# A gated cross-attention and mixture-of-experts layer: shorter gate logarithm, other places for state update and router products, idle products in the first tiles

## The chip, the core and the metric

The kernel runs on one core of a Trainium2 chip. The metric is the device time of one execution in microseconds (us); lower is better. The core has five engines with a queue each: PE (TensorE, matmuls and transposes), DVE (VectorE), ACT (ScalarE), POOL (GpSimd) and SP (SyncE, here only an issuer of DMAs). Each queue runs in order, so an instruction that waits holds up everything behind it on its engine.

## The reference, cut to what matters

Two residual layers over 8 x 512 tokens of 1024 float32 numbers. The first is an mLSTM with 16 heads of 64; q is the normalised x, k and v are the context:

```python
ig, fg = cat(q, k, v) @ Wi + bi, cat(q, k, v) @ Wf + bf      # one number a head and token
log_D = tril(cumsum(log_sigmoid(fg)) differences) + ig
D = exp(log_D - max_log_D)
C = (q k^T / 8) * D;  h = C / max(|sum C|, exp(-max_log_D)) @ v   # then a norm over each head
x = x + tanh(g_xattn) * hn
logits = layernorm(x) @ router_w.T                            # 16 experts, the best 2 of them
x = x + tanh(g_ffn) * (shared(layernorm(x)) + sum of the 2 experts)
```

`shared` and every expert are `silu(y @ gate) * (y @ up) @ down`, 1024 wide inside for the shared one and 512 for an expert.

## The kernel before, in words

Tokens go in 32 tiles of 128 (`NT = 32`), four tiles to a sequence (`NS = 4`). The work has two stages. The **loop over tiles** (the body of `flamingo_layer` from L848 on, the steps `for i in range(1, NT)`) does the mLSTM of tile i, the norm of tile i-1 and its router, and the preparation of tiles i+1 and i+2; into the gaps of PE it puts `Unit`s of the shared expert for finished tiles (`fill`, L253 gate and up products, L275 down products). The **expert stage** after it (from about 1460 us on) gathers rows by expert and multiplies (L1346). The change lies in the loop only.

A step i consists of these pieces:

- `prep_queries`, `prep_keys` (L446/L447) transpose the normalised row and the context of tile i+1; `gate_products` (L454) multiplies both by the gate weights.
- `prep_gates(i+1)`: one product `pg` (L502), then a chain on 16 x 128 numbers that goes to and fro between DVE and ACT: bias, `exp(-|f|)`, `u = 1 + z`, `ln u`, a correction by division (L519 to L527, with a RECIPROCAL at L522), two scans (`cum` L531, `m` L535) and `nm` (L539). It then writes `nm` and `e = exp(..)` to DRAM and reads them back spread over partitions: `d` (L543, L544, 128 x 2048) and, for tiles that are not the first of their sequence, `eb` (L551, L554).
- `prep_columns(i+1)` transposes the gate rows (L568, evacuated by DVE at L570), masks `d` on POOL (L573), takes `decay` out of `eb` and scales `eb` by the queries on DVE (L579, L580), and makes `wv` on POOL (L588).
- `scores`, `prep_weights` and `values` make the attention of tile i (L624, L631, L615, L652, and L646 for the state of earlier tiles). `scores`, `values` and `grow` share the two buffers of PSUM tag "a".
- `grow(i)` brings the state up to date: POOL scales it by `decay` (L667), PE makes `pst` (L675), DVE adds it (L684; L682 for a first tile). Only when DVE has read `pst` is its PSUM buffer free for the next `scores`.
- `head_scale(i)` (L692 to L700), `head_norm`, `finish_rows` end a tile; `turn_rows(i-1)` transposes the finished row into `yT` (two copies at L447, one on ACT, one on DVE); `route_products(i-1)` multiplies `yT` by the router (L454, `pp<-yT,rwT`), `finish_route` adds its parts (L745).
- Once in four tiles `place_group` computes slots and POOL issues eight indirect DMAs into `table_d` (L825).

The text order sets priorities. A scheduler fixes the order of each engine's queue at build time; `tc.issue_after(ins)` forces an instruction behind another on its engine. Before, the order on PE around the change is in most steps: `yT` transposes, one unit, router products, `values` 2 and 3, `grow` with a little of a unit between its halves, `pl`, `pc`, a unit, transposes of the next queries, `scores`.

In the first 60 us tile 0 goes through all of this with no shared expert to fill waits. Its loads are issued by SP and by ACT (L351 to L355, L395, L417, L434).

Of the kernel before, what the change touches and what calls it, by code (L numbers as in the profile page):

```python
# [9 lines left out]
F32 = mybir.dt.float32  # L10
# [36 lines left out]
def flamingo_layer(  # L47
# [274 lines left out]
    with ExitStack() as actx:  # L322
# [16 lines left out]
        def load_kv(i: int):  # L339
            q, b, c = toks[i], i // NS, i % NS  # L340
            q.kv = wk.tile([P, D], F32, tag="kv", name="kv")
            nc.sync.dma_start(q.kv, ctx_in[b, c * P : (c + 1) * P, :])
# [10 lines left out]
        bias_f = ac.tile([NH, 1], F32, name="bias_f")  # L353
        nc.scalar.dma_start(bias_i, bi.unsqueeze(1))
        nc.scalar.dma_start(bias_f, bf.unsqueeze(1))  # L355
        ones_p = ac.tile([P, P], F32, name="ones_p")
# [37 lines left out]
        lnsc = ac.tile([P, D], F32, name="lnsc")  # L394
        nc.scalar.dma_start(lnsc, ln_scale.unsqueeze(0).to_broadcast([P, D]))  # L395

# [19 lines left out]
        zeros = state.rearrange("p c e -> p (c e)")  # L416
        nc.scalar.dma_start(acc_d[T : T + P, :], zeros[:, :D])  # L417
        zero80 = ac.tile([P, NT_], F32, name="zero80")
# [12 lines left out]
        def prep_router():  # L431
            nc.vector.tensor_scalar(lnsc, lnsc, tgx, None, ALU.mult)
            rw = wk.tile([NE, D], F32, tag="u", name="rw", bufs=1)
            nc.scalar.dma_start(rw, router_w)  # L434
            nc.vector.memset(rwT, 0.0)
            prw = ps.tile([P, NC, NE], F32, tag="tr", name="prw")
            for c in range(NC):
                nc.tensor.transpose(prw[:, c, :], rw[:, c * P : (c + 1) * P], ident[:NE, :NE])
            nc.scalar.copy(rwT[:, :, 0:NE], prw)

        def transposed(dst, src_of, copies):
# [55 lines left out]
        def prep_gates(i: int, after=()):  # L497
            q, last, first = toks[i], i % NS == NS - 1, i % NS == 0
            pg = ps.tile([48, P], F32, tag="tr", name="pg")
            with ExitStack() as order:  # L500
                pinned(order, after)
                nc.tensor.matmul(pg, lhsT=sums, rhs=q.parts, start=True, stop=True)  # L502

            def row(name, bufs=2):
                return gt.tile([NH, P], F32, tag=name, name=name, bufs=bufs)

            f = row("f", 1)
            a, en, w = (rows3[i % 2][32 * k : 32 * k + NH, :] for k in range(3))
            nc.scalar.copy(f, pg[32:48, :])
            nc.vector.tensor_scalar(a, pg[0:NH, :], bias_i, None, ALU.add)  # L510
            nc.vector.tensor_scalar(f, f, bias_f, None, ALU.add)


            z, u, lnu, eq = (row(n, 1) for n in ("z", "u", "lnu", "eq"))
            nc.vector.scalar_tensor_tensor(z, f, -1.0, f, ALU.mult, ALU.min)
            nc.scalar.activation(z, z, AF.Exp)
            nc.vector.tensor_scalar(u, z, 1.0, None, ALU.add)
            nc.scalar.activation(lnu, u, AF.Ln)
            nc.vector.tensor_scalar(u, u, -1.0, None, ALU.add)  # L519
            nc.vector.tensor_scalar(eq, u, 0.0, None, ALU.is_equal)  # L520
            nc.vector.tensor_add(u, u, eq)
            nc.vector.reciprocal(u, u)  # L522
            nc.vector.tensor_mul(u, u, z)
            nc.vector.tensor_mul(lnu, lnu, u)
            nc.vector.tensor_mul(eq, eq, z)
            nc.vector.tensor_add(lnu, lnu, eq)
            nc.vector.scalar_tensor_tensor(f, f, 0.0, lnu, ALU.min, ALU.subtract)  # L527

# [33 lines left out]
            if not last:  # L562
                nc.scalar.activation(w, a, AF.Exp, bias=nm[:, P - 1 : P])

        def prep_columns(i: int):
            q, last, first = toks[i], i % NS == NS - 1, i % NS == 0
            pc = ps.tile([P, 5, NH], F32, tag="tr", name="pc")
# [3 lines left out]
            if i > 0:  # L571
# [4 lines left out]
                ).ins  # L576
            if not first:
                q.decay = sm.tile([P, NC], F32, tag="decay", name="decay", bufs=2)
                nc.vector.tensor_copy(q.decay, q.eb[:, :, P - 1])  # L579
                nc.vector.scalar_tensor_tensor(  # L580
                    q.eb, q.eb, DH**-0.5, q.qT, ALU.mult, ALU.mult
                )
            if not last:
# [152 lines left out]
        def route_products(i: int):  # L736
            q = toks[i]
            q.parts = in_groups(rwT, lambda c: q.yT[:, c, :], NC)
# [110 lines left out]
        load_kv(1)  # L849
        prep_norm(0)  # L850
        prep_queries(0)
        prep_keys(0)
# [3 lines left out]
        gate_products(0)  # L856
        prep_gates(0)
        prep_columns(0)
        with tc.issue_after(normed.last):
# [16 lines left out]
        prep_gates(1)  # L876
        grow(0)
        turn_rows(0)
        for k in range(8):
# [14 lines left out]
        for i in range(1, NT):  # L894
# [20 lines left out]
            if nxt:  # L915
                gate_products(i + 1)
            scored = scores(i, 1)
            if nxt:
                prep_gates(i + 1, scored)
# [17 lines left out]
            fill(share)  # L937
            if back:
                route_products(i - 1)
            values(i, 2)  # L940
            valued = values(i, 3)
            head_scale(i)
            if not last:
                grow(i)
            if i + 2 < NT:
                load_kv(i + 2)
            fill(share)
            if back:
                whole = finish_route(i - 1, valued)
            if nxt:  # L950
# [599 lines left out]
```

## Time and profile before

| what | us |
|---|---|
| median of 3 runs (lowest to highest) | 3169.66 (3166.38 to 3173.43) |
| the profiled execution | 3181.43 |
| its span, first to last instruction | 3179.4 |
| PE busy in the span | 3056.6 |
| DVE, ACT, POOL busy | 1793.8, 864.4, 1296.7 |
| mean granted TensorE clock | 0.978 |

The span by stage, from the busy time in stretches:

| stretch, us | length | PE busy | granted clock | DVE busy |
|---|---|---|---|---|
| 0 to 100 | 100 | 66.58 | 0.80 | 52.61 |
| 100 to 260 | 160 | 141.75 | 0.93 | 101.23 |
| 260 to 1420 | 1160 | 1114.96 | 0.97 | 777.88 |
| 1420 to 1480 | 60 | 50.17 | 0.91 | 17.69 |
| 1480 to 3179 | 1699 | 1683.16 | 1.00 | 844.42 |

Length less PE busy is time in which PE had nothing to do. Where the granted clock is under 1, PE was busy but slower: at 0.5 a matmul takes about twice as long. An "idle before, releaser" entry in a row names what ended the wait.

### The profile page before, as it was taken

The page shows a single profiled execution, that of the slowest core. Times are in us where ns is not written, and L with a number is a line of the kernel's source. Part 1 is how long each engine was busy: PE and PEld are TensorE (multiplying, and loading weights), DVE is VectorE, ACT ScalarE, POOL GpSimd, SP SyncE. Part 2 cuts the span into 40 slices and gives each one's busy share as a digit, 9 for nine tenths or more (in the row PEclk, how much of TensorE's full clock was granted, in tenths as well). Part 3 has the DMA queues.
Part 4 walks back from the last instruction along what each step waited for, and adds up shares of the span by engine and source line. Part 5 has one row for each costly group of instructions (what it writes and reads, how often), then busy time and mean ns, then how long its engine had stood idle before and what let it go on. Part 6 is the DMA issues. An engine that isn't in the chain of part 4 may idle for free.

```text
span 3179.4 us, 42509 instructions
## 1 busy us (share of the span) xinstructions
PE 3056.6 (96%) x16193; PEld 2289.5 (72%) x16193; DVE 1793.8 (56%) x3597; ACT 864.4 (27%) x1824; POOL 1296.7 (41%) x1019
## 2 busy tenths in 40 slices
PE   6889999899999999998999999999999999999999
PEld 5778677686877768676666677777777777767776
DVE  5656676676766766653444444444554554555554
ACT  3544444453545445411111111111111111100000
POOL 2212232322232222316555555565665545444442
PEclk7999999998999999999999999999999999999999
DMA  6776565565656565545544444454545544644330
GB/s 190 211 223 182 179 189 178 172 187 159 189 176 206 169 184 179 172 142 202 136 131 115 136 132 135 134 141 134 141 139 138 148 118 133 211 159 159 113 126 27
DMA packets 371103, 500.59 MB, mean 157 GB/s; under 512 B 24304, under 2 KB 263072, under 8 KB 366768
## 3 DMA queue, kind: packets, MB, share of 16 engines
q1 hardware_dynamic: 342560, 425.00, 42.2%
q0 software_dynamic: 24576, 71.52, 10.7%
q8 instruction: 130, 2.13, 0.3%
q10 hardware_dynamic: 3760, 1.31, 0.2%
q14 instruction: 77, 0.63, 0.1%
HBM read 394.57 MB, written 113.69 MB: 160 GB/s over the span
## 4 chain that ended last, share of the span: by engine, by line
PE 50%; DVE 4%; issue 0%; DVEq 0%
PE pq L1346 47%; PE ptx L1264 2%; DVE hsum L1414 1%; PE pq L1453 1%; DVE hT L1368 1%; DVE hsum L1415 1%; DVE up L1367 0%; DVE tsum L1295 0%; DVE tsum L1292 0%; DVE tsum L1293 0%; DVE yo L1425 0%; DVE xT L1267 0%; DVE u L1432 0%; DVE hT L1416 0%; DVE u L1431 0%
## 5 line engine op out<-in xcount | busy, mean ns | idle before, releaser
L1346 PE MATMUL pq<-xT,w 128*128 128x256 f32 (+12 forms) x2112 | 498.3, 386 | 9.0 <-DVEq L1327 9.0
L1346 PEld LDWEIGHTS pq<-xT,w 128*128 128x128 f32 x2112 | 402.5, 191 | 84.1 <-issue 20.2
L1346 PE MATMUL pq<-tsum,wsum 128*128 128x256 f32 (+12 forms) x1408 | 339.4, 384 | 0.0
L275 PE MATMUL pso<-sh_down,sh_hT 128*128 128x512 f32 x640 | 294.9, 605 | 2.5 <-DVE sh_base L281 2.5
L1346 PEld LDWEIGHTS pq<-tsum,wsum 128*128 128x128 f32 x1408 | 264.2, 190 | 39.7
L253 PE MATMUL pgu<-sh_yT,swg 128*128 128x256 f32 (+1 forms) x1280 | 287.5, 377 | 5.3 <-issue 4.2
L253 PE MATMUL pgu<-sh_yT,swu 128*128 128x256 f32 (+1 forms) x1280 | 285.3, 375 | 0.5 <-DMA swu<-n_L_ffn_shared_up_w_dram 0.5
L118 POOL TENSOR_SCALAR ve<-bmv 128x1 f32<-128x1 f32 x64 | 17.3, 270 | 590.8 <-DVE bmv L130 584.8
L253 PEld LDWEIGHTS pgu<-sh_yT,swg 128*128 128x128 f32 x1280 | 231.5, 193 | 36.4 <-issue 6.4
L253 PEld LDWEIGHTS pgu<-sh_yT,swu 128*128 128x128 f32 x1280 | 230.9, 192 | 31.8 <-issue 2.7
L1370 DVE TENSOR_TENSOR hT<-pq,u 128x256 f32<-128x256 f32 (+12 forms) x176 | 75.7, 430 | 300.5 <-PE pq L1346 280.7
L1311 POOL TENSOR_TENSOR wsum<-w 128x512 f32<-128x512 f32 x88 | 113.6, 1290 | 278.9 <-PE pq L1346 277.6
L275 PEld LDWEIGHTS pso<-sh_down,sh_hT 128*128 128x128 f32 x640 | 117.1, 192 | 124.7 <-issue 118.8
L1367 DVE TENSOR_TENSOR up<-pq,u 128x256 f32<-128x256 f32 (+12 forms) x176 | 75.6, 430 | 211.7 <-PE pq L1346 210.4
L1069 POOL DMA_INDIRECT acc_d<-yo,row_i x64 | 102.1, 1595 | 189.8 <-ACT yo L1443 81.5
L1346 PE MATMUL pq<-wd,hT 128*128 128x512 f32 x352 | 170.0, 598 | 7.1 <-DVE hT L1368 5.4
L1346 PE MATMUL pq<-xT,wsum 128*128 128x256 f32 (+12 forms) x704 | 169.6, 384 | 0.0
L1346 PE MATMUL pq<-tsum,w 128*128 128x256 f32 (+12 forms) x704 | 169.6, 384 | 0.0
L1346 PE MATMUL pq<-dsum,hT 128*128 128x512 f32 x352 | 165.4, 592 | 0.0
L1346 PE MATMUL pq<-dsum,hsum 128*128 128x512 f32 x352 | 165.4, 592 | 0.0
L1425 DVE TENSOR_TENSOR yo<-pq,u 128x512 f32<-128x512 f32 x176 | 119.3, 688 | 81.6 <-PE pq L1346 69.0
L1371 ACT ACTIVATE hT<-hT 128x256 f32<-128x256 f32 (+12 forms) x176 | 74.1, 421 | 327.9 <-DVE hT L1370 327.9
(274 smaller groups left out, 5462.3 us busy)
## 6 DMA issues: line engine op xcount, KB each, us to landing
swg<-L_ffn_shared_gate_w_dram SPq DMA_DIRECT2D x88, 512.0 KB, 5.2
swu<-n_L_ffn_shared_up_w_dram SPq DMA_DIRECT2D x88, 512.0 KB, 5.8
w<-in_L_ffn_gate_w_dram SPq DMA_DIRECT2D x16, 2048.0 KB, 10.8
w<-in_L_ffn_up_w_dram SPq DMA_DIRECT2D x16, 2048.0 KB, 10.6
wd<-in_L_ffn_down_w_dram SPq DMA_DIRECT2D x16, 2048.0 KB, 7.9
d<-nm_d SPq DMA_DIRECT2D x31, 1024.0 KB, 6.2
x_sb<-in_x_dram SPq DMA_DIRECT2D x32, 512.0 KB, 4.8
kv<-in_ctx_dram SPq DMA_DIRECT2D x32, 512.0 KB, 6.3
```

Source lines behind the costliest of these rows:

```text
L253: last = nc.tensor.matmul(pg[:, half, :n], lhsT=st[k][half][:, c, :], rhs=st["yT"][:, c, :n], start=(c == 0), stop=(c == NC - 1),)
L275: last = nc.tensor.matmul(po, lhsT=st["hT"][:, k, t * P : (t + 1) * P], rhs=sh_down[:, k, cols], start=(k == 0), stop=(k == 2 * NFC - 1),)
L1069: nc.gpsimd.indirect_dma_start(out=rows, out_offset=bass.IndirectOffsetOnAxis(ap=index, axis=0), in_=row, in_offset=None, compute_op=ALU.add,)
L1264: nc.tensor.transpose(pt[:, c, :], row[:, (half * 4 + c) * P : (half * 4 + c + 1) * P], ident)
L1311: nc.gpsimd.tensor_tensor(s1, a21, a22, ALU.add)
L1346: nc.tensor.matmul(out, lhsT=left[:, c, :], rhs=right[:, c, :], start=(c == 0), stop=(c == chunks - 1))
L1367: nc.vector.tensor_tensor(up, part, other, ALU.add)
L1368: nc.vector.tensor_tensor(out, out, up, ALU.mult)
L1370: nc.vector.tensor_tensor(out, part, other, ALU.add)
L1371: nc.scalar.activation(out, out, AF.Silu)
L1414: nc.vector.tensor_tensor(s1, a21, a22, ALU.add)
L1425: nc.vector.tensor_tensor(rows[t][:, halves[half]], part, other, ALU.add)
```

## The change

- **Gates.** The correction of the logarithm becomes `((u - 1) - z)`, added, with no division: three DVE instructions (new L528 to L530) in place of nine (L519 to L527); ACT adds the bias of `f` while it copies it (L518), so that one more DVE instruction goes, and the tile `eq`.
- **State inputs.** `decay` and the scaling of `eb` move from `prep_columns(i+1)`, at the end of step i, to a new `prep_state(i)` after the second half of `scores(i)`.
- **Order in a step.** `grow(i)` stands ahead of `head_scale(i)`. `route_products(i-1)` stands behind both and is forced behind the last product of `values(i, 3)`; `finish_route(i-1)` is forced behind the last unit put in (`behind`) in place of the last product of `values`.
- **Idle products.** `keep_awake(n)` issues n products of two constants, whose result nothing reads: 24 after the norm of tile 0, 26 behind `pg` of tile 0, 30 behind `pg` of tile 1.
- **Loads.** Five small loads and stores at the start go from ACT's queue to POOL's; `kv` has three buffers instead of two.

```diff
-            q.kv = wk.tile([P, D], F32, tag="kv", name="kv")
+            q.kv = wk.tile([P, D], F32, tag="kv", name="kv", bufs=3)
...
-        nc.scalar.dma_start(bias_i, bi.unsqueeze(1))
-        nc.scalar.dma_start(bias_f, bf.unsqueeze(1))
+        nc.gpsimd.dma_start(bias_i, bi.unsqueeze(1))
+        nc.gpsimd.dma_start(bias_f, bf.unsqueeze(1))
...
-        nc.scalar.dma_start(lnsc, ln_scale.unsqueeze(0).to_broadcast([P, D]))
+        nc.gpsimd.dma_start(lnsc, ln_scale.unsqueeze(0).to_broadcast([P, D]))
...
-        nc.scalar.dma_start(acc_d[T : T + P, :], zeros[:, :D])
+        nc.gpsimd.dma_start(acc_d[T : T + P, :], zeros[:, :D])
...
-            nc.scalar.dma_start(rw, router_w)
+            nc.gpsimd.dma_start(rw, router_w)
...
+        def keep_awake(n: int, after=None):
+            idle = ps.tile([P, P], F32, tag="o", name="idle")
+            with ExitStack() as order:
+                if after is not None:
+                    order.enter_context(tc.issue_after(after))
+                for _ in range(n):
+                    nc.tensor.matmul(idle, lhsT=ident, rhs=ones_p, start=True, stop=True)
...
-            nc.scalar.copy(f, pg[32:48, :])
+            nc.scalar.activation(f, pg[32:48, :], AF.Identity, bias=bias_f)
             nc.vector.tensor_scalar(a, pg[0:NH, :], bias_i, None, ALU.add)
-            nc.vector.tensor_scalar(f, f, bias_f, None, ALU.add)
...
             nc.scalar.activation(lnu, u, AF.Ln)
-            nc.vector.tensor_scalar(u, u, -1.0, None, ALU.add)
-            nc.vector.tensor_scalar(eq, u, 0.0, None, ALU.is_equal)
-            nc.vector.tensor_add(u, u, eq)
-            nc.vector.reciprocal(u, u)
-            nc.vector.tensor_mul(u, u, z)
-            nc.vector.tensor_mul(lnu, lnu, u)
-            nc.vector.tensor_mul(eq, eq, z)
-            nc.vector.tensor_add(lnu, lnu, eq)
-            nc.vector.scalar_tensor_tensor(f, f, 0.0, lnu, ALU.min, ALU.subtract)
+            nc.vector.scalar_tensor_tensor(u, u, -1.0, z, ALU.add, ALU.subtract)
+            nc.vector.scalar_tensor_tensor(f, f, 0.0, u, ALU.min, ALU.add)
+            nc.vector.tensor_sub(f, f, lnu)
...
+        def prep_state(i: int):
+            q = toks[i]
+            if i % NS == 0:
+                return
+            q.decay = sm.tile([P, NC], F32, tag="decay", name="decay", bufs=2)
+            nc.vector.tensor_copy(q.decay, q.eb[:, :, P - 1])
+            nc.vector.scalar_tensor_tensor(q.eb, q.eb, DH**-0.5, q.qT, ALU.mult, ALU.mult)
...
-            if not first:
-                q.decay = sm.tile([P, NC], F32, tag="decay", name="decay", bufs=2)
-                nc.vector.tensor_copy(q.decay, q.eb[:, :, P - 1])
-                nc.vector.scalar_tensor_tensor(
-                    q.eb, q.eb, DH**-0.5, q.qT, ALU.mult, ALU.mult
-                )
...
         prep_norm(0)
+        keep_awake(24)
...
         prep_gates(0)
+        keep_awake(26, toks[0].summed)
...
         grow(0)
+        keep_awake(30, toks[1].summed)
...
             scored = scores(i, 1)
+            prep_state(i)
...
-            if back:
-                route_products(i - 1)
             values(i, 2)
             valued = values(i, 3)
-            head_scale(i)
             if not last:
                 grow(i)
+            head_scale(i)
+            if back:
+                with tc.issue_after(valued[0]):
+                    route_products(i - 1)
...
-                whole = finish_route(i - 1, valued)
+                whole = finish_route(i - 1, behind)
```

(`toks[i].summed` is the product `pg` of tile i.)

More of the change, by code (lines that the diff above doesn't have):

```diff
@@ L501, in prep_gates @@
                 pinned(order, after)
-                nc.tensor.matmul(pg, lhsT=sums, rhs=q.parts, start=True, stop=True)
+                q.summed = nc.tensor.matmul(pg, lhsT=sums, rhs=q.parts, start=True, stop=True).ins
             def row(name, bufs=2):
@@ L508, in prep_gates @@
             a, en, w = (rows3[i % 2][32 * k : 32 * k + NH, :] for k in range(3))
-            nc.scalar.copy(f, pg[32:48, :])
+            nc.scalar.activation(f, pg[32:48, :], AF.Identity, bias=bias_f)
             nc.vector.tensor_scalar(a, pg[0:NH, :], bias_i, None, ALU.add)
-            nc.vector.tensor_scalar(f, f, bias_f, None, ALU.add)
-            z, u, lnu, eq = (row(n, 1) for n in ("z", "u", "lnu", "eq"))
+            z, u, lnu = (row(n, 1) for n in ("z", "u", "lnu"))
             nc.vector.scalar_tensor_tensor(z, f, -1.0, f, ALU.mult, ALU.min)
@@ L563, in prep_gates @@
                 nc.scalar.activation(w, a, AF.Exp, bias=nm[:, P - 1 : P])
+        def prep_state(i: int):
[5 more added lines that the diff above has]
+            nc.vector.scalar_tensor_tensor(q.eb, q.eb, DH**-0.5, q.qT, ALU.mult, ALU.mult)
         def prep_columns(i: int):
-            q, last, first = toks[i], i % NS == NS - 1, i % NS == 0
+            q, last = toks[i], i % NS == NS - 1
             pc = ps.tile([P, 5, NH], F32, tag="tr", name="pc")
```

## Prediction

> **What bounds the kernel now.** I read the stages first. From 1480 us on PE is busy for 1683.16 of 1699 us at full clock, and the change doesn't touch that code. The loop before it (0 to 1480 us) is bound by PE too: 1373.5 us busy, DVE 949, ACT 622. So an edit pays only by what PE waits, and by what it loses at a reduced clock. Busy time x (1 - granted clock), with the stage table above: 13.3 us to 100 us, 9.9 to 260, 33 to 1420. The idle time there is 33.4, 18.3 and 45.0 us.
>
> The list of who waited for whom, on PE, says for what (total us, times, longest):
>
> ```profile
> PE pt L446 <- DVE row L464: 24.2, 4, 10.0
> PE pp L454 <- ACT yT L447: 14.2, 5, 4.8
> PE psc L624 <- DVE state L684: 12.3, 7, 5.0
> PE pm L602 <- DVE nm L539: 9.1, 1, 9.1
> ...
> PE pp L454 <- DVE yT L447: 7.3, 5, 4.8
> ```
>
> The first and fourth lie in the first tiles, nearly all of them before 260 us. The router products (`pp` on `yT`) wait 14.2 + 7.3 us, 20.3 of it after 260 us. `scores` waits 12.3 us for the state. Busy time in stretches behind the larger waits shows the second price (columns: stretch, length, busy time of PE, PEld, DVE, ACT, POOL, granted clock, DMA share, GB/s):
>
> ```profile
> 738.00:748.00 10.00, 8.45 (x67) 6.04 (x68) 4.16 (x12) 2.89 (x9) 0.28 (x1) 0.66 0.77 196
> 784.00:798.00 14.00, 11.74 (x72) 9.90 (x73) 7.87 (x16) 3.98 (x9) 4.29 (x4) 0.51 0.75 215
> 956.00:970.00 14.00, 12.27 (x86) 10.70 (x87) 7.17 (x18) 4.63 (x11) 6.28 (x5) 0.63 0.91 245
> 1122.00:1134.00 12.00, 11.27 (x81) 9.63 (x82) 5.13 (x9) 2.24 (x7) 4.18 (x3) 0.57 0.76 221
> 1246.00:1256.00 10.00, 9.02 (x73) 7.52 (x74) 5.60 (x12) 2.50 (x7) 3.23 (x2) 0.66 0.76 226
> 452.00:460.00 8.00, 4.77 (x21) 3.95 (x22) 7.79 (x12) 4.71 (x16) 4.77 (x2) 0.57 0.70 195
> 622.00:632.00 10.00, 7.32 (x17) 3.46 (x18) 6.79 (x14) 0.00 (x0) 4.84 (x2) 0.66 0.28 105
> 22.50:53.30 30.80, 23.70 (x137) 21.44 (x137) 12.47 (x47) 11.80 (x32) 4.48 (x5) 0.51 0.51 153
> ```
>
> The first five follow waits of the router products (2.18, 4.82, 4.80, 4.05 and 1.88 us): 2.9 + 5.8 + 4.5 + 4.8 + 3.1 = 21.1 us lost to the clock. The next two follow waits for the state (4.95, 3.83): 2.1 + 2.5 = 4.6.
>
> In order of time, one of each kind:
>
> ```profile
> 782.90 0.81 DVE L464 TENSOR_SCALAR row<-x_sb,bmv,rstd 128x1024 f32<-128x1024 f32 x1 [4.37 <-POOL rstd L121]
> 785.51 0.69 DVE L447 COPY yT<-pt 128x512 f32<-128x512 f32 x1
> 786.26 0.65 PE L454 MATMUL pp<-yT,rwT 128*32 128x128 f32 x8 [4.82 <-DVE yT L447]
> ...
> 450.28 0.40 DVE L579 COPY decay<-eb 128x8 f32<-128x8 f32 x1 [5.87 <-DMA eb<-e_d]
> 454.90 0.76 PE L624 MATMUL psc<-qT,kT 64*128 64x128 f32 x2 [4.95 <-DVE state L684]
> ...
> 620.75 0.42 DVE L684 TENSOR_TENSOR state<-state,pst 64x260 f32<-64x260 f32 x1 [5.78 <-POOL state L667]
> ```
>
> At 782.9 DVE had stood behind POOL, which issued eight indirect DMAs (0.97 us each and 0.30 between) before its part of the norm; `yT` was queued behind. At 450 DVE stood at `decay` until the DMA of `eb` landed, with the state update behind it. At 620 POOL had waited 10.2 us for the DMA of `d`, with the scaling of the state behind it.
>
> **Router products.** They move behind `values` 2 and 3 and the first half of `grow`. In the changed order of PE this holds in nearly every step ("values, grow, one router product, grow, the rest"). The work put ahead of them is 2.7 us (770.38 to 773.1) + 0.7 for half of `grow`: 3.4 us of cover, against a longest wait of 4.8. The rest goes because `yT` itself comes sooner where the gate chain stands ahead of it on DVE (next point; at 786 the norm's row is now queued behind the chain, so that from its end to that of the copy it is 0.7 us instead of 2.5). What is late next is `grow`, which needs the PSUM buffers of `values` evacuated by ACT (0.4 us each); ACT's `e`, ahead of that in its queue, is out by then in most steps. Of 20.3 + 21.1 = 41.4 us I take nine tenths: -37. Nothing else is queued behind the moved products that was ahead of them, except `pc`, whose PSUM buffer comes free with a copy of 0.26 us.
>
> Here the Trainium skill ("TensorE: Matmul & The Clock Gate", The HAM clock gate and HAM oscillation) speaks against so large a sum: it gives about 3.4 us of idleness as the limit for PE, so that the waits of 2.18 and 1.88 us would cost only themselves, 6 us less. The rows of 738 and 1246 show 0.66 behind just these, so I keep them.
>
> **Gates.** The removed DVE instructions measure 0.266 (L511), 0.218, 0.215, 0.277, 0.940 (the RECIPROCAL), 0.267, 0.275, 0.216, 0.274, 0.276 us = 3.22; the three added are of the same forms, 0.83. So 2.4 us a tile, 77 us of DVE in all. DVE is no bound (777.88 of 1160 us), so this alone is worth nothing, but behind `ln` the chain shrinks from 2.96 us to 0.27. In tile 0 that is on the path (`pm` waits for `nm`): -2.5. The bias on ACT rides on a copy that is there anyway (0.26 us; bounds -0.05 and +0.1 a tile, hidden by the 2 us of PE work queued there: 0).
>
> **State.** `grow` ahead of `head_scale` spares the update a reduction (1.21 us) queued between. But the changed order has two things the other way. POOL's mask of `d`, which waits for a DMA, stands ahead of the scaling of the state in 11 of the 16 tiles concerned (7 before), and DVE's `decay`, although written later in the text, is queued ahead of the state update in 6 tiles (2 before). Before, `d` landed 7 to 9.5 us after `nm`, in two tiles 13.2 and 13.6; `eb`, where waited for, 8 to 17 us after `e`; `scores` needs the state some 12 to 20 us after. Two gaps from 7 tiles, at (8.8 + 4.6) / 2 = 6.7 us each, make 3.1 gaps from 11: +7.5. Bounds: -13.4 if the shorter chain sends the DMAs early enough for all, +60 if nine more gaps open; the old rate is the nearest row.
>
> **First tiles.** A product of 128 x 128 takes 0.23 us at full clock and 0.43 at half (16 records, two a product: 1.87 against 3.48 us). The 26 and 30 products thus take 6.1 to 11.3 and 7.0 to 13.1 us, in waits of 9.1 (less 2.5) and 8.4 us. Started cold they overrun by 2 us or so each: the clock came back 4.6 to 5.3 us after dense work began at 155 and 65.6. In exchange the clock may hold where it was 0.51 (22.5 to 53.3): 23.70 x 0.49 = 11.6 us. The rule just named, that some 3.4 us of activity release the clock, would leave only 1.7 us to win there; the row shows half clock through over 20 us of unbroken but thin work (products of 16 and 64 rows). I take half, -5.8, since ACT's 16 exponentials (4.6 us) and DVE lie across it. For 60 to 72 us, clock 0.57 and 6.36 us busy, I take 1.5 of 2.7. The 24 products before the first row take 5.6 to 10.4 us in a wait of 8.4. The clock's row reads 1.00 there, but the eight transposes at 10 us took 1.97 us and those at 83 us 1.04, so PE starts at half clock: 0.9 won against an overrun of up to 2: 0.
>
> **Loads on POOL.** No direct DMA of POOL is in the trace. Nearest row: its indirect ones, 1.27 us with the gap. Four stand ahead of the first norm, 5.1 us in an idle stretch of 3.4, and one inside it: up to +3.0; at SP's 0.4 each, 0. Against that the first copy of `qT` (13.77) no longer waits behind ACT's issues, 1.8 us. Net 0, bounds -1.8 and +1.2. `kv` with three buffers lets SP issue it without waiting for `grow`: -0 to -2 (the waits on `kv` were 0.9 us on PE): -0.5.
>
> **100 to 260 us.** The steps with few units wait for latencies; units move from one side of `scores` to the other. Waits for `yT` and state (0.9, 1.6, 1.2, and a clock of 0.5 after the second) say -3, bounds -10 and +6.
>
> **Sum.** -37 - 2.5 + 7.5 - 5.8 - 1.5 - 0.5 - 3 = -42.8. The profiled execution took 3181.4 us (span 3179.4), 11.8 over the median: it would take 3138.6, and the median 3127. I shade it by 4 us for DVE's evacuation of `pc`, which now stands behind the state (the waits on `cols` were 4.0 us): **3131**.
>
> **Rivals.**
> - *Half the gain.* In the steps with the eight indirect DMAs (786, 957, 1122) POOL still holds the norm for 10 us, ACT's `e` behind it holds the evacuation of `values`, and PE waits at `grow` instead. Then 13.7 us of waits and 15.1 of clock come back: -14, 3156. For it: ACT stood 5.8 and 7.05 us at `e` there. Against: cover and shorter chain together exceed 4.8 us. 0.20.
> - *More.* The clock holds through tile 0 and no state gap is left: -42.8 - 7.5 - 13.4 - 5.8 = -69.5, 3104 with the shading. 0.12.
> - *Slower.* The DMAs of `d` and `eb` land behind the need for the state on DVE's and POOL's queues, 6.7 us a gap. The -50 of all else is used up from eight gaps more than before; with ten of the tiles concerned, +17: 3187. For it: the orders named, and `eb` at 8 to 17 us. Against: five of seven such tiles had no gap. 0.13.
> - *It does not do what it says*: idle products run cold into the work behind them, +5; it stays inside the forecast.
>
> **Chances and range.** Forecast 0.55 (3113 to 3150). About 0.2%, 6.3 us, is what a measurement can tell from no change. Faster 0.79 (forecast, second rival and 0.12 of the first), same 0.06 (of the first), slower 0.15 (the third, and 0.02 of the first). Range 3104 to 3176.
>
> **What would show it.** In the profile after: no wait of `pp` on `yT` over 1 us after 260 us, and the clock at 1.00 at these steps; DVE about 77 us less busy; waits of `psc` for the state and of DVE for `eb` no larger than 12 and 35 us (if they double, the third rival); waits of `pst` for ACT or POOL in the steps with indirect DMAs (the first). The clock from 22 to 55 us tells of the idle products. I am wrong if `d` and `eb` land late in most tiles.

## The result: 0.5% slower, and the profile after

| | before | after |
|---|---|---|
| median of 5 runs (lowest to highest), us | 3172.32 (3166.38 to 3173.43) | 3189.51 (3181.20 to 3196.31) |
| the profiled execution, its span | 3181.43, 3179.4 | 3196.31, 3194.6 |
| PE, DVE busy | 3056.6, 1793.8 | 3070.5, 1710.5 |
| first product of the expert stage starts at | 1457.91 | 1472.84 |

The ratio is 1.0049, 95% interval 1.0035 to 1.0064: some 15 us slower (a thousandth is 3.2 us). Nearly all of it was lost in the loop: the expert stage starts 14.9 us later, and the span is 15.2 us longer.

The list of waits on PE, after (total us, times, longest):

```profile
PE pt L455 <- DVE nrm L701: 18.7, 4, 6.8
PE pt L455 <- DVE decay L574: 16.5, 2, 9.1
PE pt L455 <- DVE row L473: 13.9, 3, 5.7
PE pso L275 <- DVE sh_base L281: 11.0, 3, 4.7
PE psc L630 <- DVE state L690: 8.4, 6, 3.3
PE pt L455 <- DVE cols L582: 4.8, 3, 2.7
...
PE pp L463 <- DVE yT L456: 3.5, 1, 3.5
```

The router's waits fell from 21.5 us to a single one of 3.5 (at 1307 us), and those of `scores` for the state from 12.3 to 8.4. In their place stand transposes (`pt`) that wait for DVE. For `nrm` and `cols` they wait 23.5 us, against 4.0 before. Units of the shared expert wait 11.0 us for DVE to evacuate their product (`sh_base`), 2.5 before. The two waits put down to `decay`, 16.5 us, are waits for the norm's `row`: at 243.53 `pt` started 0.15 us after `row` ended, with a `decay` of 0.17 us begun in between; with `row` itself that makes 30.4 us, 24.2 before. The clock moved with the waits. Stretches of the kernel after behind the waits of 9.11, 6.79 and 5.74 us, then the first tile, then the three stages (columns as before):

```profile
244.00:258.00 14.00, 13.36 (x90) 11.22 (x89) 10.32 (x13) 7.39 (x20) 0.79 (x2) 0.80 0.23 71
466.00:480.00 14.00, 13.23 (x92) 9.67 (x94) 9.77 (x21) 8.59 (x21) 4.81 (x2) 0.81 0.31 85
794.00:808.00 14.00, 13.84 (x98) 10.10 (x99) 5.77 (x7) 3.46 (x7) 5.00 (x3) 0.82 0.81 264
22.50:53.30 30.80, 29.10 (x188) 25.55 (x187) 13.74 (x46) 11.72 (x32) 4.80 (x6) 0.64 0.55 163
...
0.00:100.00 100.00, 86.81 (x683) 77.91 (x684) 50.93 (x126) 38.30 (x83) 24.80 (x70) 0.81 0.69 200
100.00:260.00 160.00, 133.90 (x1117) 109.94 (x1117) 95.90 (x189) 70.87 (x165) 36.98 (x29) 0.93 0.68 204
260.00:1420.00 1160.00, 1101.26 (x7509) 862.78 (x7508) 691.28 (x1557) 500.76 (x1113) 303.65 (x260) 0.97 0.60 178
```

Against the stage table of before: PE's idle time is 20.2 us less up to 100 us, 7.9 more to 260 and 13.7 more to 1420, +1.3 in all. PE's busy time over the whole span rose by 13.9, which the 80 idle products more than account for (18.4 us by an estimate, at the 0.23 us of a product at full clock). The two sums make the 15.2. So the idle products filled the early gap without shortening it, and the later stages gained gaps; the clock of 260 to 1420 is 0.97 as before, since new waits reduce it as the old ones did.

### The profile page after: what moved, and what is told of

It reads as the page before. It is cut to its first block, busy times and chain, and to the rows that moved or that the text cites. A ratio compares the mean times of both kernels' runs of the same rounds, so it can differ in the third digit from the quotient of the medians.

```text
span 3194.6 us, 42655 instructions
## 1 busy us (share of the span) xinstructions
PE 3070.5 (96%) x16353; PEld 2306.9 (72%) x16353; DVE 1710.5 (54%) x3373; ACT 862.0 (27%) x1819; POOL 1300.6 (41%) x1024
## 4 chain that ended last, share of the span: by engine, by line
PE 49%; DVE 4%; issue 0%; DVEq 0%
PE pq L1357 47%; PE ptx L1275 2%; DVE hsum L1425 1%; PE pq L1464 1%; DVE hT L1379 1%; DVE hsum L1426 1%; DVE up L1378 0%; DVE tsum L1306 0%; DVE tsum L1304 0%; DVE tsum L1303 0%; DVE yo L1436 0%; DVE xT L1278 0%; DVE u L1443 0%; DVE hT L1427 0%; DVE u L1442 0%
## 5 line engine op out<-in xcount | busy, mean ns | idle before, releaser
L118 POOL TENSOR_SCALAR ve<-bmv 128x1 f32<-128x1 f32 x64 | 14.9, 233 | 545.8 <-DVE bmv L130 524.7
```

## One gap, followed through

The transposes of tile 11 wait 6.79 us at 459.97 to 466.77. From the timeline of the kernel after (start, length, engine, operation, in brackets the idle time before it and its releaser):

```profile
455.53 0.29 PE L580 MATMUL pc<-ident,rows 80*128 80x80 f32 x1
...
456.81 2.01 POOL L585 TENSOR_SCALAR_AFFINE_SELECT d<-d 128x2048 f32<-128x2048 f32 x1 [7.03 <-DMA d<-nm_d]
...
458.79 3.27 POOL L673 TENSOR_TENSOR state<-state,decay 64x520 f32<-64x520 f32 x2
...
459.09 0.80 DVE L574 COPY decay<-eb 128x8 f32<-128x8 f32 x1 [7.31 <-DMA eb<-e_d]
...
463.07 1.73 DVE L690 TENSOR_TENSOR state<-state,pst 64x260 f32<-64x260 f32 x4
...
466.42 0.20 DVE L582 COPY cols<-pc 128x48 f32<-128x48 f32 x1
...
466.77 0.45 PE L455 MATMUL pt<-ident,row 128*128 128x128 f32 x1 [6.79 <-DVE nrm L701]
```

`pc` was done at 455.8, but `cols`, the copy that empties its PSUM buffer, stood on DVE behind the state update, and this behind `decay`, which waited 7.31 us for the DMA of `eb`, a value that the *next* tile needs. On POOL the mask waited 7.03 us for the DMA of `d`, with the scaling of the state behind it. `pt` shares the two buffers of tag "tr" with `pc`: it started 0.15 us after `cols` ended. The trace names `nrm`, which ended in between and which `pt` doesn't read; several short instructions of DVE end just ahead of `pt` here, and the name given is that of the last of them. Before, the same `eb` was waited for at 450, ahead of the same update, and `scores` paid 4.95 us. So this gap shows how the order costs; the change added others of its kind (counted at the end).

In totals, the DVE waits of before and after:

```profile
DVE decay L579 <- DMA eb<-e_d: 34.5, 9, 5.9
DVE state L684 <- POOL state L667: 9.2, 4, 5.8
```

```profile
DVE decay L574 <- DMA eb<-e_d: 39.0, 11, 8.0
DVE state L690 <- POOL state L673: 29.3, 16, 6.6
```

and POOL's for the DMA of `d` went from 134.8 us in 18 waits to 207.0 in 26.

## The experiments

All times are compared with the kernel before, run on the same chip beside each; "us" in the last column is (ratio - 1) x 3170. Differences between two rows have a half-width of some 5 to 9 us. A name in `route_` is the router edit in the kernel before and something else, one in `rg_` the router edit and the gate edit.

| kernel | ratio (95%) | us |
|---|---|---|
| the changed kernel | 1.0049 (1.0035 to 1.0064) | +15.5 |
| gates_alone | 1.0022 (1.0011 to 1.0033) | +7.0 |
| idle_alone | 1.0004 (0.9992 to 1.0016) | +1.3 |
| old_gates | 1.0010 (0.9995 to 1.0024) | +3.2 |
| decay_late | 1.0000 (0.9991 to 1.0010) | 0 |
| mask_late | 1.0064 (1.0046 to 1.0083) | +20.3 |
| both_late | 0.9958 (0.9940 to 0.9975) | -13.3 |
| both_cols | 0.9961 (0.9949 to 0.9973) | -12.4 |
| route_alone | 0.9923 (0.9902 to 0.9944) | -24.4 |
| route_gates | 0.9968 (0.9953 to 0.9983) | -10.1 |
| route_loads | 0.9964 (0.9951 to 0.9977) | -11.4 |
| route_pool | 0.9922 (0.9903 to 0.9940) | -24.7 |
| route_stsw | 0.9953 (0.9937 to 0.9970) | -14.9 |
| route_idle | 0.9943 (0.9923 to 0.9962) | -18.1 |
| route_forced | 0.9945 (0.9928 to 0.9963) | -17.4 |
| rg_decay | 0.9974 (0.9964 to 0.9983) | -8.2 |
| rg_forced | 0.9965 (0.9952 to 0.9978) | -11.1 |
| rg_masknorm | 0.9989 (0.9978 to 1.0000) | -3.5 |
| rg_all_late | 0.9953 (0.9937 to 0.9968) | -14.9 |

**First: which part, and is it the order of the queues?** Theory A: the shorter gate chain lets the scheduler put DMA-waiting instructions (`decay`, the mask) ahead of others. Theory B: the router products' new place. Theory C: the idle products.

*gates_alone*: the gate edit of the diff, alone, in the kernel before.

> The kernel before with the gate edit alone (three DVE instructions for nine, bias on ACT). Theory A (order): the shorter chain lets the scheduler queue decay and the mask of d, which wait for DMAs, ahead of the state update and of cols (decay ahead of the update in 8 tiles instead of 2, the mask ahead of the state's scaling in 11 instead of 7), so this alone is slower, by 10 to 25 us. Theory B (router products): the loss comes from the router products' new place, so this is the same as before within 6 us or a little faster. Theory C (idle products): the same as before.

Measured +7.0 us: a cut of some 80 us of DVE work made the kernel slower, by less than theory A expected. In the order that the scheduler fixed, `decay` now stands ahead of the state update in 8 tiles (2 before) and ahead of `cols` in 16 (5), without any other part of the change.

*old_gates*: the changed kernel with the gates of before.

> The changed kernel with the old gates (division, bias on DVE), all else as changed. Theory A: the order of decay and mask is then nearly that of before (1 and 5 tiles), the router products no longer wait, so it is faster than before by 10 to 30 us. Theory B or C: still slower than before, by 10 to 20 us.

Measured +3.2, no difference to before, and in neither expected range: without the gate edit the other parts do *not* give the forecast gain. The gates alone were not the answer.

*decay_late*: the changed kernel, `decay` and `eb` forced behind the last DVE instruction of the step's own scores.

```diff
-            nc.vector.tensor_copy(q.decay, q.eb[:, :, P - 1])
-            nc.vector.scalar_tensor_tensor(q.eb, q.eb, DH**-0.5, q.qT, ALU.mult, ALU.mult)
+            with tc.issue_after(q.scored):
+                nc.vector.tensor_copy(q.decay, q.eb[:, :, P - 1])
+                nc.vector.scalar_tensor_tensor(q.eb, q.eb, DH**-0.5, q.qT, ALU.mult, ALU.mult)
```

> The changed kernel with decay and the scaling of eb forced behind the last score product of their own step on DVE (no tile has them ahead of the state update or of cols). The mask on POOL stays ahead in 11 tiles. Theory A: the waits of PE behind decay (16.5 us) and part of those behind nrm and cols (23 us) go: 15 to 35 us faster than the changed kernel, so 0 to 20 us faster than before. Theory B or C: no more than 5 us from the changed kernel.

Measured 0: 15.5 us less than the changed kernel, at the low end of theory A's 15 to 35. The place of this one pair of instructions is worth that.

*idle_alone*: the three `keep_awake` calls alone in the kernel before.

> The kernel before with the 24 + 26 + 30 idle products alone. Theory A and B: the clock holds or not in the first 60 us, 0 to 8 us faster than before, nothing after 100 us. Theory C (the idle products run into the work behind them): 5 to 15 us slower than before, all of it before 100 us.

Measured +1.3, within its interval nothing: theory C is out, in both directions.

**Second: the router alone, and POOL's queue.** *route_alone*: the router edit alone in the kernel before. *mask_late*: the changed kernel with the mask behind the step's last POOL operation of the norm. *both_late*: that and decay_late. *both_cols*: that and `cols` copied by ACT.

```diff
-            if back:
-                route_products(i - 1)
             values(i, 2)
...
+            if back:
+                with tc.issue_after(valued[0]):
+                    route_products(i - 1)
...
-                whole = finish_route(i - 1, valued)
+                whole = finish_route(i - 1, behind)
```

```diff
             if i > 0:
+                with ExitStack() as order:
+                    if i > 1:
+                        order.enter_context(tc.issue_after(toks[i - 1].scaled))
-                q.cut = nc.gpsimd.affine_select(
+                    q.cut = nc.gpsimd.affine_select(
...
-            nc.gpsimd.tensor_tensor(q.scale, var, mhalf, ALU.pow)
+            q.scaled = nc.gpsimd.tensor_tensor(q.scale, var, mhalf, ALU.pow).ins
...
-            nc.vector.tensor_copy(q.cols, pc[:, 0:5:2, :])
+            nc.scalar.copy(q.cols, pc[:, 0:5:2, :])
```

> The kernel before with the router edit alone: the router products behind values 3, and their last product behind the unit put in. No other part of the change. Theory A (the change loses because the shorter gate chain puts DVE's decay and POOL's mask, both waiting for a DMA, ahead of other work): the order of decay and mask stays as before here (decay ahead of the state update in 2 tiles), so the forecast gain of the router waits should show: 10 to 30 us faster than before, 3142 to 3162, with no wait of pp for yT over 1 us. Theory B (the new place of the router products is itself the loss: what was covered by them now waits for cols or nrm): not faster than before, 3170 to 3190, and PE waits of pt for nrm or cols appear that before did not have.

> The changed kernel with POOL's mask of d forced behind the last POOL operation of the step's own norm (hrstd), so that it stands ahead of the scaling of the state in no tile (11 in the changed kernel); decay stays where the changed kernel has it. Theory A gives the mask a part of the loss of its own: 3175 to 3184, 5 to 15 us below the changed kernel, DVE's wait of state for POOL falls from 29.3 us to under 15. If the mask is harmless: within 3 us of the changed kernel, 3187 to 3193.

> The changed kernel with both forced: decay and eb behind the step's own scores on DVE, the mask behind hrstd on POOL. No DMA wait stands ahead of a state update. Theory A: the two parts add, 3160 to 3170, faster than the kernel before by 2 to 12 us. Rival B (the new place of the router products costs what it gains): no better than 3173, the time with decay late alone. Waits of pt for a norm's row, 31 us with decay late alone, should fall under 15 if the mask made them.

> As both_late, and the evacuation of pc (cols) on ACT in place of DVE, so that the PSUM buffer which the next transposes need does not come free behind the state update on DVE. If the waits of pt for cols, nrm and the like are what is left of the loss: 3 to 8 us below both_late. If ACT's queue, where e and the evacuations of values stand, is no better place: within 2 us of both_late, and waits of pt for ACT appear.

route_alone took 24.4 us off (interval 18 to 31): theory B is out, and the largest term of the prediction was sound in kind. Its waits on PE:

```profile
PE pt L446 <- DVE row L464: 22.7, 4, 9.9
...
PE pst L675 <- issue: 8.2, 4, 4.8
PE pt L446 <- DVE cols L570: 8.1, 5, 4.4
...
PE pp L454 <- ACT yT L447: 2.2, 1, 2.2
```

Of the waits for `yT` one of 2.2 us is left (at 933), and `cols` (8.1 us, 4.0 before) and `pst` (16.0 in all, 3.7 before) took up part of them. One of the `pst` waits, 4.82 us at 769.87, is in a step with the indirect DMAs and as long as the router's was there. ACT stood at `e`, and the evacuations of `values` behind it; then the clock in the 14 us behind the wait:

```profile
767.82 0.40 ACT L550 ACTIVATE e<-m 16x128 f32<-16x128 f32 x1 [7.34 <-DVE m L535]
...
769.87 1.14 PE L675 MATMUL pst<-wv,kv 128*64 128x65 f32 x16 [4.82 <-issue]
...
770.00:784.00 14.00, 14.00 (x109) 11.65 (x110) 6.92 (x19) 4.17 (x8) 6.79 (x3) 0.83 1.02 295
```

That is the first rival, in a step of its own.

mask_late changed nothing (+4.8 against the changed kernel, inside the two intervals): an expectation of theory A that failed. both_late took 28.8 us off the changed kernel, 13.3 beyond decay_late. The two waits are parallel ways to the same state update, and with one of them gone the other still holds it. The state update of the gap above in decay_late and the transposes behind it, then `decay` and the transposes in mask_late:

```profile
449.62 0.42 DVE L690 TENSOR_TENSOR state<-state,pst 64x260 f32<-64x260 f32 x1 [4.32 <-POOL state L673]
...
454.03 1.09 PE L455 MATMUL pt<-ident,row 128*128 128x128 f32 x4 [3.63 <-DVE nrm L701]
```

```profile
449.67 0.17 DVE L573 COPY decay<-eb 128x8 f32<-128x8 f32 x1 [5.97 <-DMA eb<-e_d]
...
455.85 0.63 PE L455 MATMUL pt<-ident,row 128*128 128x128 f32 x4 [3.94 <-DVE nrm L702]
```

Only with both gone does the gap close. The same place in both_late:

```profile
441.81 0.20 DVE L582 COPY cols<-pc 128x48 f32<-128x48 f32 x1
...
442.15 0.63 PE L455 MATMUL pt<-ident,row 128*128 128x128 f32 x4 [0.31 <-DVE nrm L703]
...
445.34 2.02 POOL L587 TENSOR_SCALAR_AFFINE_SELECT d<-d 128x2048 f32<-128x2048 f32 x1
```

0.31 us in place of 6.79, with the same named releaser, and a mask that waits for no DMA at all. both_cols is level with both_late: with the waiters gone, where `cols` runs doesn't matter.

The forcing took away what it aimed at: the waits for `nrm` and `cols`, for `sh_base` and of `scores` for the state, 42.9 us together in the changed kernel, are 1.6 in both_late. The waits for the norm's `row` stayed:

```profile
PE pt L455 <- DVE row L473: 34.6, 5, 10.0
...
PE pt L455 <- DVE nrm L703: 0.3, 1, 0.3
```

They were expected to fall under 15. All but 3.9 us of them lie after 100 us, where the kernel before has 5.8.

**Third: what do the other parts cost beside the router edit?** Each is the router edit and one other part of the diff: the gates (route_gates), the idle products (route_idle), the five DMAs on POOL with three `kv` buffers (route_loads), the new places of `decay`/`eb` and of `grow` (route_stsw).

> The kernel before with the router edit and the gate edit alone. The router edit alone took 26 us off, the gate edit alone put 7 on; yet the changed kernel stands 17 above before, so that about 36 us come from the two together or from the rest (idle products, loads, state inputs, grow ahead of head_scale). If the two add up: 3152, 19 below before, and the 36 us are the rest's. If they work against each other (decay is queued ahead of the state update in 6 tiles and ahead of cols in 15, as in the changed kernel, and with the router products gone from behind the transposes nothing covers the wait for cols): 3175 to 3189.

> The kernel before with the router edit and the idle products. Idle products alone were worth 0. If they are harmless here too: 3145, as the router edit alone (within 5 us). If they are part of the 36 us (they fall into the first tiles and shift the time at which units of the shared expert start): 3150 to 3165.

> The kernel before with the router edit, the five small DMAs on POOL and three buffers for kv. The prediction held these at nothing. If that holds: 3145 within 5 us. If three kv buffers let SP issue loads earlier and these stand ahead of the DMAs of d and eb on SP's queue: 3150 to 3170, with DVE's wait for eb or POOL's for d larger than with the router edit alone.

> The kernel before with the router edit, decay and eb taken at the new place in the text, and grow ahead of head_scale. The order of decay, mask and state is that of before (decay ahead of the state in 2 tiles). If these edits are harmless: 3145 within 5 us. If grow ahead of head_scale is what leaves transposes waiting for nrm and row (the DVE chain of the norm now stands behind the state update, which waits for PE): 3155 to 3175, with PE waits of pt for nrm above 5 us.

Over route_alone the gates cost 14.3 us, the loads 13.0, the state edits 9.5, the idle products 6.3 (its interval includes nothing). -24.4 + 14.3 + 13.0 + 9.5 + 6.3 = +18.7, against +15.5 measured for all together. This sum is a weak test: route_alone stands in it several times, so that its half-width is some 22 us, and one of the losses, that of the loads, has in part a cause that the changed kernel doesn't meet (below). Every part but the router's is a loss or nothing. The gates cost 7.0 us alone; that it is more here is inside the uncertainty.

**Fourth: the loads, and the gates' 14 us.** *route_pool* is route_loads with two `kv` buffers. *route_forced* is the router edit with the orders of both_late; *rg_forced* adds the gate edit; *rg_decay* is rg_forced without the mask's order.

> The kernel before with the router edit and the five small DMAs on POOL; kv keeps two buffers. With both, the gate weights landed 2.7 us later than with the router edit alone (14.5 against 11.8 us), since the large loads of POOL went out ahead, and DVE took the mean of the next kv, which waited 4.7 us for its DMA, ahead of tile 0's gate chain; nm of tile 0 was 8.3 us later. If the places on POOL cost only the 2.7: 3146 to 3150, and the rest of the 13 us is the third kv buffer's. If all is POOL's: 3155 to 3160.

> The kernel before with the router edit, decay and eb forced behind the step's own scores, and the mask forced behind hrstd. If waits for DMAs on the queues of DVE and POOL cost the router edit alone something too: 3130 to 3140, below its 3145. If the forcing only repairs what the gate edit does to the order: 3142 to 3150.

> The kernel before with the router edit and the gate edit, with decay, eb and the mask forced late. Theory A: the gate edit's 13 us on top of the router edit come from the order of decay and mask, so with the order forced it costs nothing: 3135 to 3147. If the shorter chain costs by itself (by other moves of the scheduler): it stays at 3153 to 3160.

> As rg_forced, with decay and eb forced late alone; the mask stays where the scheduler puts it (ahead of the scaling of the state in 11 tiles or so). Theory A, from the changed kernel, where decay late alone took 16 us off and the mask 18 more: halfway, 3145 to 3152. If decay is the whole cost of the gate edit: as rg_forced.

route_pool costs nothing (-24.7, as the router alone): the 13 us are the third `kv` buffer's. With it, the load of tile 2's `kv` no longer waits for a buffer (issued at 28.16 us, in place of 59.42), the mean over it stands earlier in DVE's queue, and DVE meets it inside the gate chain of tile 0. DVE in route_loads, then in route_pool:

```profile
29.55 0.27 DVE L524 TENSOR_TENSOR lnu<-lnu,u 16x128 f32<-16x128 f32 x1
34.55 1.22 DVE L478 TENSOR_REDUCE vmean<-kv 128x16 f32<-128x1024 f32 x1 [4.73 <-DMA kv<-in_ctx_dram]
35.69 0.27 DVE L526 TENSOR_TENSOR lnu<-lnu,eq 16x128 f32<-16x128 f32 x1
...
37.52 0.21 DVE L539 TENSOR_SCALAR nm<-m 16x128 f32<-16x128 f32 x1
```

```profile
29.57 0.27 DVE L524 TENSOR_TENSOR lnu<-lnu,u 16x128 f32<-16x128 f32 x1
29.89 0.27 DVE L526 TENSOR_TENSOR lnu<-lnu,eq 16x128 f32<-16x128 f32 x1
...
31.71 0.21 DVE L539 TENSOR_SCALAR nm<-m 16x128 f32<-16x128 f32 x1
```

`nm`, for which PE waits there, is 5.8 us later. The rest of the 13 us is not located. This is the same thing as at 450: an instruction that waits for a DMA stands in an in-order queue ahead of one that could run. In the changed kernel itself this place is not hit (its shorter chain is through before; `nm` starts at 27.91); in old_gates it is (35.66), so old_gates mixes two things. The changed kernel stands 12.3 us above it, near the 14.3 of the gate edit beside the router edit.

rg_forced fell short of theory A: with the orders of both_late the gate edit still stands where route_gates does (-11.1 and -10.1). rg_decay (-8.2) is level with both: here `decay` late gives nothing, with or without the mask. In rg_forced PE waits for the norm's `row`; one of three such places:

```profile
224.72 2.91 POOL L699 TENSOR_TENSOR hrstd<-var,mhalf 128x16 f32<-128x16 f32 x1 [9.50 <-DVE var L697]
227.60 2.00 POOL L578 TENSOR_SCALAR_AFFINE_SELECT d<-d 128x2048 f32<-128x2048 f32 x1
229.58 1.93 POOL L587 TENSOR_TENSOR wv<-v,cols 128x1040 f32<-128x1040 f32 x1
231.47 0.22 POOL L118 TENSOR_SCALAR ve<-bmv 128x1 f32<-128x1 f32 x1
231.78 0.56 POOL L121 TENSOR_TENSOR rstd<-ve,mhalf 128x1 f32<-128x1 f32 x1
...
232.38 0.81 DVE L464 TENSOR_SCALAR row<-x_sb,bmv,rstd 128x1024 f32<-128x1024 f32 x1 [5.16 <-POOL rstd L121]
...
233.33 1.94 PE L446 MATMUL pt<-ident,row 128*128 128x128 f32 x8 [6.52 <-DVE row L464]
```

Mask and `wv`, 3.9 us, stand ahead of two short instructions of the next norm, for which PE waits. In the queue's order the mask does so in no step of the kernel before or of the router edit alone; in route_gates and rg_forced in three (2, 4 and 17), in the changed kernel in four (3 as well).

The changed kernel's two longest waits for `row`, at 156.64 and 243.53, have another cause, although the mask stands ahead there too: POOL had finished the mask (and `wv`) when `var`, the input of its `hrstd`, came; `hrstd` started 0.08 us after `var` ended, and the norm stood behind its 2.91 us. Around 243 in the changed kernel, then the transposes there in route_stsw and in route_alone:

```profile
237.31 1.38 DVE L704 SCALAR_TENSOR_TENSOR var<-var,nrm 128x16 f32<-128x16 f32 x1
...
238.77 2.91 POOL L706 TENSOR_TENSOR hrstd<-var,mhalf 128x16 f32<-128x16 f32 x1
```

```profile
234.76 1.51 PE L446 MATMUL pt<-ident,row 128*128 128x128 f32 x6 [6.01 <-DVE row L464]
```

```profile
226.22 1.94 PE L446 MATMUL pt<-ident,row 128*128 128x128 f32 x8 [2.18 <-DVE row L464]
```

In route_stsw the mask stands ahead of the norm in no step, and the two waits are 6.79 and 6.01 us against 2.25 and 2.18 in route_alone. So they come with the state edits, which queue the state update ahead of the chain that ends in `var`. How much of the 9.5 us of these edits the two waits make is not shown, nor which of the two edits it is.

**Fifth: the mask behind the norm.** Mask and `wv` were moved into a function of their own, after `prep_norm(i + 2)`, and forced behind its `rstd`; in *rg_masknorm* alone with the router and gate edits, in *rg_all_late* together with the orders of rg_forced.

```diff
             if i + 2 < NT:
                 prep_norm(i + 2)
+            if nxt:
+                prep_mask(i + 1)
...
+                    if i + 1 < NT:
+                        order.enter_context(tc.issue_after(toks[i + 1].normed))
```

> The kernel before with the router edit and the gate edit, with POOL's mask and wv forced behind the rstd of the next norm, so that they stand ahead of it in no tile (in 3 or 4 tiles with the two edits alone, in none before); decay where the scheduler puts it. If these tiles are the gate edit's cost: 3143 to 3150, against 3157 with the two edits alone. If decay, queued ahead of row in the same places, holds the row by itself: 3153 to 3159, and PE still waits about 6 us there.

> As before, with all three orders forced: decay and eb behind the step's scores, the mask behind hrstd and behind the rstd of the next norm. Against rg_forced (3158) this differs by the last alone. If the mask ahead of the norm is what was left: 3143 to 3152, and the waits of 4.7, 6.5 and 3.1 us for the row become some 2 us. If it stays within 3 us of 3158, no order of the three waiters explains the gate edit's cost, and it stays open.

rg_masknorm is slower than route_gates (by 6.6 us): a miss. rg_all_late is 3.8 us below rg_forced, inside the uncertainty; its waits of 4.7, 6.5 and 3.1 us for the row became 3.9, 4.3 and none. With all three orders forced the gate edit costs 2.5 us (rg_all_late against route_forced), which is nothing that these runs can tell; but the forcing itself costs the router edit 7 (half-width 9). So **the gate edit's 14 us are not settled**: they vanish only between two kernels that are both worse than the router edit alone (route_forced lies above both of its expected ranges), and no single order of the three gives them back.

No version measured beats the router edit alone (or with the DMAs on POOL): 0.8% faster than before, and 1.3% faster than the changed kernel.

## Why the prediction was wrong, point by point

- **Router products, -37 of 41.4: right in kind, too large.** Alone they gave -24.4. The waits for `yT` went as said, but for one of 3.5 us, and with them the lower clock *at these waits*. What came in their place was the first rival (waits of `pst` in the steps with indirect DMAs, and a clock of 0.83 behind one of them, where 1.00 was forecast) and `cols`. That rival was set up as all or nothing; it was a share of the truth.
- **"Two gaps from 7 tiles ... make 3.1 gaps from 11: +7.5 ... the old rate is the nearest row." This is the step that failed.** The orders named there (mask ahead of the state in 11 tiles, `decay` ahead in 6) were read rightly, and forcing them away takes 28.8 us off the changed kernel. The rate was taken over the steps with the mask ahead, and `decay`, ahead in 6 steps in place of 2, got no price. In the profile of the changed kernel PE has gaps of over 2 us behind a late state update in seven steps, where the kernel before has two (9 and 13) and the forecast had 3.1. They make 30.8 us of waits: in five of the six steps with `decay` ahead (6, 9, 10, 21 and 24: 3.28, 6.79, 3.16, 4.30 and 3.66 us), but only in two of the six with the mask alone (13 and 18: 5.71 and 3.92). Such a step cost PE what it had cost before, 4.4 us of wait on average; it was the number of steps that was wrong. In both_late no gap over 2 us is left in the seven. The upper bound of +60 held it. This is not the whole miss: with both orders forced the changed kernel is 13.3 us faster than before, where 39 was forecast. The other terms follow.
- **The place of the loss.** The text expected late states to show at `scores`, and gave two signs: waits of `psc` under 12 us and of DVE for `eb` under 35. They came out at 8.4 and 39.0, so nearly as in the good case. The loss came out further back in DVE's queue: `cols`, behind the state on DVE, held the transposes. The text had this ("I shade it by 4 us"); the waits for `nrm` and `cols` measured 23.5 us against 4.0, those for `sh_base` 11.0 against 2.5. The name of a wait moves with the order, and a sign has to cover every instruction behind the late one.
- **Gates, "alone is worth nothing", -2.5 in tile 0.** The DVE saving was 83 us, near the 77 worked out, and tile 0's `nm` did come 3.7 us sooner in gates_alone (25.6 against 29.3). The net was +7.0 alone and +14.3 beside the router edit. The text charged the *state* term for the changed order and took the gate term as free; it was the gate edit that changed the order.
- **"`grow` ahead of `head_scale` spares the update a reduction": counted as a help.** Beside the router edit the state edits cost 9.5 us, and the norm's `row` came late behind them. The text weighed what the update no longer waits for and, but for `cols`, not what now waits for the update.
- **Loads, "Net 0", `kv` -0.5: wrong by 13.** POOL's issues took 0.55 to 0.74 us, not 1.27, and the gate weights were used 2.6 us later (14.51 against 11.92), beyond the bound of +1.2, but route_pool says that this costs nothing. The third buffer, put down as a small gain, cost the 13 beside the router edit, 5.8 of them by an order that was open to be read: the text went through DVE's queue around the state, not in tile 0.
- **First tiles, -5.8 and -1.5: nothing gained.** PE was busy for 29.10 of 30.80 us at 22.5 to 53.3 and the clock was 0.64: 10.5 us lost, against 11.6 before. The prediction doubted the rule of 3.4 us there and was right to doubt it, but still booked half.
- **Third rival, "Slower", 3187 at 0.13.** It named the mechanism and, within 3 us, the time. The second is luck: it let all other terms come true (-50) and laid +67 of late states on top, where the router gave 24 and the other parts lost. Its "Against: five of seven such tiles had no gap" used the old kernel's rate as evidence for an order that the old kernel did not have.

## What to carry to other kernels

Shortening a chain is not free where a scheduler fixes the order: what becomes ready earlier by its reckoning is queued earlier, and if that is an instruction that waits for a DMA, everything behind it on that engine waits too. List, for the changed order, each instruction that waits for a DMA and all that stands behind it until the next one needed by PE; and don't price a new order at the old order's rate. Take such a change apart before taking it: here one edit of five held the gain, and the other four gave it all back.

## What had not been expected of the hardware

- PE at work did not bring the clock back: over the 30.8 us of tile 0 that are shown it was busy 94% of the time, with full 128 x 128 products ahead of it and in it, at a granted clock of 0.64. In both_late, with the same idle products, the row of the same stretch reads 0.87, and in route_alone, which has none, 0.67: a single execution says little of it, and no effect of the idle products on the clock is shown. The Trainium skill ("TensorE: Matmul & The Clock Gate", The HAM clock gate) would have PE at full clock after some 3.4 us of activity; the row differs.
- A direct DMA issue on POOL took 0.55 to 0.74 us (five of them in route_loads), about half of what its indirect ones take (0.97 and a gap of 0.30).
- The first issue of a large load at 3.3 us in place of 9.3 (`lnsc`, 512 KB) came with a landing of the gate weights 2.7 us later, though they were issued first and on other queues. Five DMAs were moved at once; which of them did it was not run.
